# Moving openings, squares and normalising between the slots of a graph-attention layer, and regrouping its first two groups' loads

## The chip, the cores and the metric

The kernel runs on one NeuronCore of a Trainium2 chip. Its engines work from queues of their own, each in order: TensorE (PE in the profile; PEld are its weight loads) does matrix products into PSUM, VectorE (DVE) and ScalarE (ACT) read and write PSUM and SBUF, GpSimd (POOL) works on SBUF only, and SyncE (SP) issues nearly all DMA transfers. The metric is the device time of one execution in microseconds. Three executions before the change took 2890.96, 2896.06 and 2899.04 us; the median is 2896.06. The profiled execution is a fourth one.

## The reference

x has 128 graphs of 128 nodes and 768 features, adj is 128 x 128 x 128. All data are float32.

```python
h = jnp.maximum(_layernorm(x), 0.0)              # over the features, no weights
q, k, v = (split_heads(h @ W + b) for W, b in ((Wq, bq), (Wk, bk), (Wv, bv)))   # 12 heads of 64
scores = einsum('bhqd,bhkd->bhqk', q, k) / sqrt(64) + beta * adj
scores = where(adj > 0, scores, -9e15)
out = einsum('bhqk,bhkd->bhqd', softmax(scores), v)
return x + out
```

## The kernel before

**Groups.** Four graphs make a group; there are 32 groups, 0 to 31. The activations of a group, normalised and transposed (`to_hT`, line 439), lie in six tiles A00 to A12: r (0 or 1) is a pair of graphs, the second digit a third of the features. The weights fall into blocks B00 to B22, and the output of each projection into keys (r, j), two by three. There are three slices of products per group: `qk0` (heads 0 to 5 of q and k), `v`, and `qk1` (heads 6 to 11).

**Group 0** uses plain products (`plain_slice`): 18 slots a slice, each with four products of 256 columns; three slots (k = 0, 1, 2) fill one key, and its PSUM pair is then evicted (line 820 for q and k, line 812 for v, where VectorE adds V's bias). While it runs, VectorE, GpSimd and ScalarE also make the weight sums for the later groups (`prepare`, lines 266 to 296, two steps a slot); each is stored to DRAM (`kept_*`, line 272, SP's queue) from a ring of five buffers, except twelve that stay in SBUF. The raw weights of `qk1` overwrite those of `qk0` in the big tile `sbig`, by eight transfers at V's slot 5 (`raw_qk`). The ring later holds the T tiles that `load_T` (line 319) brings back.

**Groups 1 to 31** use a fast scheme (`product_z`, line 530): 15 products a slice instead of 18, each of seven zones with two halves, from sums of activations (`sum_acts`, line 444, VectorE; `inner`, lines 449 to 451, GpSimd) and the prepared weights T. Products belong to four chains a, b, c, d; a chain accumulates in one PSUM pair, and the running sum is read after each of its products. So the next product of a chain waits for the readings of the one before. The first reading for a key is its *opening*: for q and k three ScalarE instructions (lines 548 and 550), for V five zones by ScalarE (line 544) and then two zones with the bias by VectorE (line 545). Every further reading is a VectorE addition into the key's tile `home` (line 554). When a key is complete, GpSimd decodes it (`decode`): lines 570 to 573 for q and k, 581 to 585 for V.

**Slots.** A slot is one product with what is emitted behind it. The order on every engine is written out by hand: `then(n, f)` puts f behind the product of slot n and ahead of its readings; `then((n, "post"), f)` behind its readings; `trailing` runs between the two; `later(f, s)` defers by s slots. An engine executes its instructions in the order of emission, so an instruction that waits holds back all that were emitted later on that engine.

**What else fills the slots.** `scores` (line 607) multiplies q and k for two heads, VectorE masks (615), ScalarE takes the exponential (617). `attend` (660) multiplies by V; its products are put between the zones of the next slot's product; ScalarE copies (669) and divides (643), VectorE adds x (676). `bias_steps` prepares the mask of the next group in four steps: VectorE transposes adj (467), ScalarE squares it (468) for a range test, VectorE takes the maximum (470) and finishes the mask (472, 473, 475). `norm` (428) is the layer norm's last step on ScalarE, four instructions per graph, from moments that `half_stats` (401) takes on halves of rows that `load_half` (393) loads, and `row_moments` turns through DRAM (413, 417, 418).

**Waiting for the first activations.** For group 1 the moments come from `stats` (344) and two small products (355, 369) in group 0's V slice. For group 2 the eight half rows are loaded and measured from slot 8 of group 0's `qk1` slice to slot 6 of group 1's `qk0` slice, all through one buffer (`if G == 2 or n % 3 == 2`), since the other two lie where group 1's x is kept until then.

Of the kernel before, what the change touches and what calls it, by code (L numbers as in the profile page):

```python
# [17 lines left out]
P = 128  # L18
# [107 lines left out]
def direct(ctx, tc, x, adj, wq, bq, wk, bk, wv, bv, beta, out, bad):  # L126
# [39 lines left out]
    def flat(lo, hi):  # L166
        return sbig[:, lo:hi]
# [36 lines left out]
    ones = const.tile([P, 1], F32, name="ones")  # L204
# [24 lines left out]

    def raw_qk(u, t, parts, engines=(nc.sync, nc.sync)):  # L230
# [5 lines left out]
        for k in range(3):  # L236
            for j in range(3):
                wt[f"qk{u}", f"B{k}{j}"] = v[:, 2 * k:2 * k + 2, :, j]
# [166 lines left out]
    def row_moments(G):  # L405
# [11 lines left out]
        later(lambda: nc.sync.dma_start(turned.rearrange("i b s -> b i s"), t.rearrange("p s g -> p (s g)")), 5)  # L417
        later(lambda: nc.sync.dma_start(to.rearrange("p b s g -> p (b s g)"),
                                        turned.rearrange("i b s -> i (b s)")[None].to_broadcast([NB, SQ, NB * 2 * GRP])), 8)
# [43 lines left out]
    def bias_steps(G):  # L463
# [4 lines left out]
        nc.scalar.activation(raw, raw, AF.Square, scale=beta_s)  # L468
# [45 lines left out]
    def product_z(G, sl, n):  # L514
# [21 lines left out]
        for (r, j), sign in uses:  # L536
            key = (G, sl, r, j)
            op = ALU.add if sign > 0 else ALU.subtract
            if key not in qk:
                left[key] = sum(k == (r, j) for q in PRODUCTS for k, _ in q[3])  # L540
                t = qk[key] = home_qk(*key, zones=True)
                if sl == "v":
                    bias = bv_b[:, j * 2 * P:(j + 1) * 2 * P].rearrange("p (i n) -> p i n", i=2)
                    nc.scalar.activation(t[:, 0:5], p[:, 0:5], AF.Copy, scale=float(sign))
                    nc.vector.tensor_tensor(t[:, 5:7], bias, p[:, 5:7], op)  # L545
# [230 lines left out]
    def plain_slice(G, sl, todo, rows=(0, 1)):  # L776
# [3 lines left out]
        for r in rows:  # L780
            for j in range(3):
# [5 lines left out]
                for at, k in [(at, k) for at in parts for k in range(3)]:  # L787
                    a, b = A[G, f"A{r}{k}"], wt[sl, f"B{k}{j}"]
                    for i in range(2):
                        for c in range(2):  # L790
# [10 lines left out]
                            turn()  # L801
                    if at is not parts[-1]:
# [4 lines left out]
                    if k == 2:  # L807
                        if sl == "v":
                            t = vt[G, sl, r, j] = vring[nv[0] % len(vring)]
                            nv[0] += 1  # L810
                            bias = bv_b[:, j * 2 * P:(j + 1) * 2 * P].rearrange("p (h d) -> p h d", d=HD)
                            nc.vector.tensor_tensor(
                                t.rearrange("p (g h) e -> p g h e", g=2)[:, :, :, 0:HD],
                                bias[:, None, :, :].to_broadcast([P, 2, 4, HD]),
                                p.rearrange("p g (h d) -> p g h d", d=HD), ALU.add)
# [413 lines left out]
```

## Time and profile before

| | |
|---|---|
| median of three runs | 2896.06 us |
| the profiled execution | 2880.61 us, its span 2878.5 us |
| busy: TensorE, VectorE, ScalarE, GpSimd | 2709.7, 2351.4, 1494.1, 2167.5 us |
| DMA | 707.01 MB, mean 246 GB/s, mean share of the engines 82.3% on the main queue |
| granted TensorE clock, mean | 0.993 |
| first product of group 1 | starts at 139.86 us |

Read the table with care: TensorE's 94% is an average over a start in which it often stands and 29 alike groups in which it stands for short, regular gaps. In the groups of lines "idle before" is the time in which an engine stood before that instruction, and the name behind the arrow is what it waited for last. In the stage rows the columns are the stretch, its length, the busy time (and number of instructions) of PE, PEld, DVE, ACT and POOL, the granted clock, the DMA share and GB/s. A row of waits gives the waiting engine, tile and line, what it waited for, the total, the number of times and the longest. A row of the timeline gives start, duration, engine, line, operation, tiles and shape, the number of instructions merged in it, and in brackets the idle time before it and what ended that.

### The profile page before, as it was taken

The page shows a single profiled execution, that of the slowest core. Times are in us where ns is not written, and L with a number is a line of the kernel's source. Part 1 is how long each engine was busy: PE and PEld are TensorE (multiplying, and loading weights), DVE is VectorE, ACT ScalarE, POOL GpSimd, SP SyncE. Part 2 cuts the span into 40 slices and gives each one's busy share as a digit, 9 for nine tenths or more (in the row PEclk, how much of TensorE's full clock was granted, in tenths as well). Part 3 has the DMA queues.
Part 4 walks back from the last instruction along what each step waited for, and adds up shares of the span by engine and source line. Part 5 has one row for each costly group of instructions (what it writes and reads, how often), then busy time and mean ns, then how long its engine had stood idle before and what let it go on. Part 6 is the DMA issues. An engine that isn't in the chain of part 4 may idle for free.

```text
span 2878.5 us, 121298 instructions
## 1 busy us (share of the span) xinstructions
PE 2709.7 (94%) x52005; PEld 2564.9 (89%) x52005; DVE 2351.4 (82%) x3218; ACT 1494.1 (52%) x3812; POOL 2167.5 (75%) x3152
## 2 busy tenths in 40 slices
PE   8789999999999999999999999999999999999998
PEld 7588999999988999889999899999899898999997
DVE  6778888888888788888888888888888888888885
ACT  2256555556454555545565545555555555555644
POOL 3648787778787778777787877787877787777875
PEclk9899999999999999999999999999999999999999
DMA  8688888888888888888888888888888888888875
GB/s 202 197 247 256 242 260 261 254 251 251 242 253 253 257 244 235 258 254 251 254 255 240 257 258 252 256 250 242 257 256 254 247 235 256 261 256 258 238 220 156
DMA packets 543010, 707.01 MB, mean 246 GB/s; under 512 B 107388, under 2 KB 406152, under 8 KB 542472
## 3 DMA queue, kind: packets, MB, share of 16 engines
q1 hardware_dynamic: 541312, 698.45, 82.3%
q8 instruction: 411, 6.73, 0.9%
q10 hardware_dynamic: 1160, 0.79, 0.1%
q14 instruction: 127, 1.04, 0.1%
HBM read 633.51 MB, written 65.59 MB: 243 GB/s over the span
## 4 chain that ended last, share of the span: by engine, by line
PE 42%; POOL 20%; DVE 11%; issue 5%; DMA 2%; ACT 2%; SPq 1%; POOLq 0%; DVEq 0%; ACTq 0%
PE pair L530 34%; DVE home L554 5%; PE pair L607 4%; PE pair L660 4%; POOL v L585 4%; POOL home L583 3%; DMA x<-in_x_dram 2%; POOL v L584 2%; POOL home L582 2%; POOL home L570 2%; POOL v L581 1%; DVE strow L401 1%; POOL A L449 1%; DVE e L615 1%; POOL home L573 1%
## 5 line engine op out<-in xcount | busy, mean ns | idle before, releaser
L554 DVE TENSOR_TENSOR home<-home,pair 128x896 f32<-128x896 f32 x798 | 846.7, 1071 | 202.3 <-PE pair L530 156.6
L530 PE MATMUL pair<-sbig,T_qk 128*64 128x128 f32 x14756 | 954.9, 274 | 16.4 <-ACT e L669 6.8
L530 PEld LDWEIGHTS pair<-sbig,T_qk 128*64 128x64 f32 x14756 | 804.7, 137 | 35.1 <-issue 27.2
L643 ACT ACTIVATE e<-e,sm 128x64 f32<-128x64 f32 x1512 | 382.4, 336 | 289.8 <-DVE sm L631 289.8
L530 PE MATMUL pair<-T_v,sbig 128*64 128x128 f32 x7812 | 458.9, 273 | 3.2 <-DVE home L545 1.4
L530 PEld LDWEIGHTS pair<-T_v,sbig 128*64 128x64 f32 x7812 | 430.5, 137 | 12.8 <-issue 6.2
L660 PE MATMUL pair<-v,e 128*64 128x65 f32 x6048 | 406.5, 222 | 37.3 <-POOL v L585 25.6
L660 PEld LDWEIGHTS pair<-v,e 128*64 128x64 f32 x6048 | 356.6, 137 | 55.4 <-POOL v L585 32.9
L570 POOL TENSOR_TENSOR home<-home 128x256 f32<-128x256 f32 x319 | 307.0, 962 | 65.9 <-DVE home L554 62.9
L449 POOL TENSOR_TENSOR A<-A 128x256 f32<-128x256 f32 x186 | 142.0, 763 | 267.6 <-DVE A L439 267.6
L530 PE MATMUL pair<-A,T_qk 128*64 128x128 f32 x4340 | 337.8, 273 | 5.3 <-issue 5.3
L617 ACT ACTIVATE e<-e 128x1024 f32<-128x1024 f32 x189 | 200.0, 1058 | 230.2 <-DVE e L615 229.9
L530 PE MATMUL pair<-A,res_qk 128*64 128x128 f32 x4340 | 265.6, 273 | 36.6 <-ACT home L550 32.1
L548 ACT ACTIVATE home<-pair 128x640 f32<-128x640 f32 x319 | 224.1, 703 | 134.6 <-PE pair L530 131.8
L530 PEld LDWEIGHTS pair<-A,res_qk 128*64 128x64 f32 x4340 | 238.9, 137 | 44.1 <-ACT home L550 38.6
L428 ACT ACTIVATE x<-x,block 128x192 f32<-128x192 f32 x480 | 231.8, 540 | 81.2 <-DMA x<-in_x_dram 80.3
L573 POOL TENSOR_TENSOR home<-home 128x256 f32<-128x256 f32 x319 | 244.4, 766 | 25.0
L571 POOL TENSOR_TENSOR home<-home 128x256 f32<-128x256 f32 x319 | 237.1, 743 | 25.0
L669 ACT COPY e<-pair 128x520 f32<-128x520 f32 x189 | 111.4, 590 | 256.2 <-PE pair L660 256.2
L530 PEld LDWEIGHTS pair<-A,T_qk 128*64 128x64 f32 x4340 | 237.7, 137 | 7.0 <-issue 7.0
L615 DVE SCALAR_TENSOR_TENSOR e<-pair,biasT 128x1024 f32<-128x1024 f32 x189 | 227.1, 1202 | 4.6 <-PE pair L607 4.2
L572 POOL TENSOR_TENSOR home<-home 128x128 f32<-128x128 f32 x319 | 201.1, 630 | 25.0
(180 smaller groups left out, 4495.2 us busy)
## 6 DMA issues: line engine op xcount, KB each, us to landing
T_qk<-kept_qk SPq DMA_DIRECT2D x682, 448.0 KB
T_v<-kept_v SPq DMA_DIRECT2D x341, 448.0 KB
xo<-in_x_dram SPq DMA_DIRECT2D x189, 256.0 KB
out_dram<-xo SPq DMA_DIRECT2D x189, 256.0 KB
x<-in_x_dram SPq DMA_DIRECT2D x248, 192.0 KB
sbig<-in_x_dram SPq DMA_DIRECT2D x180, 192.0 KB
half<-in_x_dram SPq DMA_DIRECT2D x66, 192.0 KB
kept_qk<-prep_qk SPq DMA_DIRECT2D x22, 448.0 KB
```

The costliest lines, as they stand in the source:

```text
L428: nc.scalar.activation(t, t, AF.Relu, bias=shift[G, n], scale=rstd[G, n])
L530: nc.tensor.matmul(p[q:q + HD, at, :], lhs[:, q:q + HD], rhs, start=(first and at % 4 == 0), stop=True, skip_group_check=True)
L548: nc.scalar.activation(t[:, 0:5], p[:, 0:5], AF.Copy, scale=float(sign))
L554: nc.vector.tensor_tensor(t, t, p[:, 0:7], op)
L570: e.tensor_tensor(t[:, 1:4:2], t[:, 1:4:2], twice(5), ALU.add)
L571: e.tensor_tensor(t[:, 2:5:2], t[:, 2:5:2], twice(1), ALU.add)
L572: e.tensor_tensor(t[:, 4], t[:, 4], t[:, 6], ALU.add)
L573: e.tensor_tensor(t[:, 0:7:6], t[:, 0:7:6], twice(2), ALU.add)
L615: nc.vector.scalar_tensor_tensor(e, ps, SCORE_CAP * ISCALE, bias, op0=ALU.min, op1=ALU.add)
L617: trailing.append(lambda: nc.scalar.activation(e, e, AF.Exp, scale=1.0 / ISCALE))
L643: nc.scalar.activation(o[:, r, b, 0:HD], pa[:, r, b, 0:HD], AF.Copy, scale=t[:, 1, r, b:b + 1])
L660: nc.tensor.matmul(pa[q:q + HD, 2 * g + i, :], k[:, q:q + HD], vt[G, "v", r, h // 4][:, 4 * g + h % 4, :], start=True, stop=True, skip_gro ...
```

## The change

It has three groups of parts.

In every group from 1 on: VectorE's part of V's opening is emitted ahead of ScalarE's; the square of adj goes to `trailing`, behind the slot's openings. In groups 2 to 29, which prepare a next group from the second on: the normalising of graphs 2 and 3 of the next group moves from V's slots 0 to 3 to slots 5, 6, 8 and 9, and the transposition and inner sums of A11 from slot 6 to slot 12. In `qk1` the second and third attend move from slots 7 and 10 to 8 and 11.

In group 0: V's bias comes into PSUM by a product of one row of ones with one row of the bias, two such products per key, and ScalarE evicts by a plain copy; the ones become a 128 x 128 tile. The eight raw loads of `qk1` are issued one a slot, slots 5 to 12. The moments of group 1 move from slots 8 and 10 to 9 and 12, its normalising and first transpositions a slot back.

In groups 0 and 1: group 2's half rows are all loaded and measured in group 1's `qk0` slice, through three buffers, the moments' turn through DRAM follows in fewer slots, and group 2's first two graphs are normalised whole at V's slots 2 and 3.

```diff
-    ones = const.tile([P, 1], F32, name="ones")
+    ones = const.tile([P, P], F32, name="ones")
...
+    def raw_qk1_piece(at):
+        v = flat(0, RAW).rearrange("p (c i n) -> p c i n", c=NC, i=2)
+        a, i = at // 2, at % 2
+        nc.sync.dma_start(v[a * SQ:(a + 1) * SQ, :, i], rows_of[("q", "k")[i]][a][:, :, 3 * P:6 * P])
+        if not at:
+            name_raw(1, flat(0, RAW).rearrange("p (c i j n) -> p c i j n", c=NC, i=2, j=3))
...
-        if G == 2 or n % 3 == 2:
+        if n % 3 == 2:
...
-        nc.scalar.activation(raw, raw, AF.Square, scale=beta_s)
+        trailing.append(lambda: nc.scalar.activation(raw, raw, AF.Square, scale=beta_s))
...
+                    nc.vector.tensor_tensor(t[:, 5:7], bias, p[:, 5:7], op)
                     nc.scalar.activation(t[:, 0:5], p[:, 0:5], AF.Copy, scale=float(sign))
-                    nc.vector.tensor_tensor(t[:, 5:7], bias, p[:, 5:7], op)
...
+                    if sl == "v" and k == 0:
+                        for i in range(2):
+                            nc.tensor.matmul(p[:, i], ones[0:1], bv_b[0:1, j * 2 * P:(j + 1) * 2 * P], start=False,
+                                             stop=True, skip_group_check=True)
...
-                            bias = bv_b[:, j * 2 * P:(j + 1) * 2 * P].rearrange("p (h d) -> p h d", d=HD)
-                            nc.vector.tensor_tensor(
-                                t.rearrange("p (g h) e -> p g h e", g=2)[:, :, :, 0:HD],
-                                bias[:, None, :, :].to_broadcast([P, 2, 4, HD]),
-                                p.rearrange("p g (h d) -> p g h d", d=HD), ALU.add)
+                            nc.scalar.copy(t.rearrange("p (g h) e -> p g h e", g=2)[:, :, :, 0:HD],
+                                           p.rearrange("p g (h d) -> p g h d", d=HD))
...
-        then(12 + g, norm, 1, g)
-    then(5, lambda: raw_qk(1, flat(0, RAW), ((0, 3),)))
+        then(13 + g, norm, 1, g)
+    for n in range(8):
+        then(5 + n, raw_qk1_piece, n)
...
-    then(8, lambda: mom.extend(moments_1(1, 0, GRP * NB)))
-    then(10, lambda: moments_2(1, 0, GRP * NB, *mom))
+    then(9, lambda: mom.extend(moments_1(1, 0, GRP * NB)))
+    then(12, lambda: moments_2(1, 0, GRP * NB, *mom))
...
-    turn_act(1, ((2, "A01"), (3, "A02"), (4, "A00"), (9, "A10"), (10, "A11"), (11, "A12")))
+    turn_act(1, ((3, "A01"), (4, "A02"), (5, "A00"), (9, "A10"), (10, "A11"), (11, "A12")))
...
-    for n, at in enumerate((8, 10, 12, 14, 16)):
-        then((at, "post"), load_half, 2, n)
-    for n, at in enumerate((10, 12, 14, 16)):
-        then(at, half_stats, 2, n)
...
-            for n, at in enumerate((0, 2, 4, 6)):
-                then(at, half_stats, 2, 4 + n)
-                if n:
-                    then((at - 2, "post"), load_half, 2, 4 + n)
-            then(7, row_moments, 2)
+            for n, at in enumerate((0, 0, 0, 3, 4, 5, 6, 7)):
+                then((at, "post"), load_half, 2, n)
+            for n, at in enumerate((3, 4, 5, 6, 7, 8, 9, 10)):
+                then(at, half_stats, 2, n)
+            then(10, row_moments, 2, 3, 5)
...
-            for g in range(2):
-                for h in range(2):
-                    then((2 * g + h, "post"), norm, G + 1, g + (G > 1) * 2, 2 * h, 2 * h + 2)
             if G == 1:
+                for g in range(2):
+                    then((2 + g, "post"), norm, 2, g)
                 turn_act(2, ((5, "A01"), (6, "A00"), (7, "A02"), (14, "A11")))
...
             else:
-                turn_act(G + 1, ((6, "A11"),))
+                for n, at in enumerate((5, 6, 8, 9)):
+                    then((at, "post"), norm, G + 1, 2 + n // 2, n % 2 * 2, n % 2 * 2 + 2)
+                turn_act(G + 1, ((12, "A11"),))
...
-        attention(G, 0, ((3, 2), (7, 1), (10, 0)))
+        attention(G, 0, ((3, 2), (8, 1), (11, 0)))
```

`row_moments` takes the two delays (5 and 8 slots before) as arguments, and `raw_qk`'s naming of the blocks becomes `name_raw`.

More of the change, by code (lines that the diff above doesn't have):

```diff
@@ L228, in load_cols, with name_raw @@
             engine.dma_start(t[a * SQ:(a + 1) * SQ], rows_of[name][a][:, chunks, at:at + t.shape[-1]])
+    def name_raw(u, v):
+        for k in range(3):
+            for j in range(3):
+                wt[f"qk{u}", f"B{k}{j}"] = v[:, 2 * k:2 * k + 2, :, j]
     def raw_qk(u, t, parts, engines=(nc.sync, nc.sync)):
@@ L403, in half_stats, with row_moments @@
             nc.vector.bn_aggr(rows[G, "mv"][:, g, :], rows[G][:, g])
-    def row_moments(G):
+    def row_moments(G, first=5, then=8):
         mv = rows[G, "mv"]
@@ L416, in row_moments @@
         turned = dram.tile([SQ, NB, 2 * GRP], F32, name=f"turned_{G}")
[L417 removed]
+        later(lambda: nc.sync.dma_start(turned.rearrange("i b s -> b i s"), t.rearrange("p s g -> p (s g)")), first)
         later(lambda: nc.sync.dma_start(to.rearrange("p b s g -> p (b s g)"),
[L419 removed]
+                                        turned.rearrange("i b s -> i (b s)")[None].to_broadcast([NB, SQ, NB * 2 * GRP])), then)
         for g in range(GRP):
@@ L1096, in direct @@
     pf = take()
-    nc.tensor.matmul(pf[0:1, 0, 0:NS + 24], ones, over, start=True, stop=True)
+    nc.tensor.matmul(pf[0:1, 0, 0:NS + 24], ones[:, 0:1], over, start=True, stop=True)
     nc.vector.tensor_reduce(bad, pf[0:1, 0, 0:NS + 24], AX.X, ALU.max)
```

4 lines of the change are left out of this document (1 added, 3 removed).

## The prediction

> **What bounds the kernel now.** I read the page first, then the busy time by stages, the waits, and the timeline.
>
> ```profile
> span 2878.5 us, 121298 instructions
> PE 2709.7 (94%) x52005; PEld 2564.9 (89%) x52005; DVE 2351.4 (82%) x3218; ACT 1494.1 (52%) x3812; POOL 2167.5 (75%) x3152
> ...
> PE 42%; POOL 20%; DVE 11%; issue 5%; DMA 2%; ACT 2%; SPq 1%; POOLq 0%; DVEq 0%; ACTq 0%
> ```
>
> TensorE is busy 94%, but the chain that ended last is TensorE for only 42%; 20% is GpSimd. So there is a GpSimd chain inside the groups. The stages, by columns of length, busy time per engine, clock, DMA share:
>
> ```profile
> 0.00:139.80 139.80, 115.55 (x847) 92.12 (x847) 96.77 (x220) 33.75 (x88) 71.85 (x132) 0.94 0.72 196
> 139.80:242.70 102.90, 87.00 (x1645) 83.15 (x1647) 79.83 (x119) 53.20 (x142) 58.26 (x89) 0.92 0.86 254
> 242.70:2772.20 2529.50, 2414.83 (x47682) 2303.38 (x47680) 2107.32 (x2772) 1358.90 (x3455) 1977.04 (x2842) 1.00 0.85 251
> ```
>
> Group 0 takes 139.8 us and group 1 102.9, both with a reduced clock; the 29 groups after them 87.2 each. What waits:
>
> ```profile
> POOL A L449 <- DVE A L439: 267.6, 91, 5.2
> ACT adj L468 <- DVE biasT L467: 266.8, 32, 9.7
> DVE home L545 <- ACT home L544: 160.4, 109, 3.8
> ACT x L428 <- DMA x<-in_x_dram: 80.3, 30, 3.8
> ```
>
> Three of them are queue heads that hold back something else: the square (L468) and the normalising (L428) sit before openings on ScalarE, and L545 keeps VectorE waiting for L544. Where this reaches TensorE, group 14's timeline shows:
>
> ```profile
> 1335.59 0.42 DVE L545 TENSOR_TENSOR home<-bv_b,pair 128x256 f32<-128x256 f32 x1 [2.26 <-ACT home L544]
> 1336.06 1.75 PE L530 MATMUL pair<-res_v,A 128*64 128x128 f32 x28 [0.29 <-DVE home L545]
> 1346.39 0.46 POOL L581 TENSOR_TENSOR v<-home 128x128 f32<-128x128 f32 x1 [3.08 <-DVE home L554]
> 1353.53 0.72 ACT L468 ACTIVATE adj<-adj,beta_s 128x512 f32<-128x512 f32 x1 [9.74 <-DVE biasT L467]
> 1356.53 1.75 PE L530 MATMUL pair<-A,res_qk 128*64 128x128 f32 x28 [1.97 <-ACT home L550]
> 1363.91 1.23 POOL L584 TENSOR_TENSOR v<-sbig 128x128 f32<-128x128 f32 x1
> 1364.85 1.23 DVE L444 TENSOR_TENSOR sbig<-A,sbig 128x896 f32<-128x896 f32 x1
> 1366.72 0.34 PE L660 MATMUL pair<-v,e 128*64 128x65 f32 x4 [0.73 <-POOL v L585]
> 1383.76 0.45 PE L607 MATMUL pair<-home 64*64 64x128 f32 x8 [0.30 <-POOL home L573]
> ```
>
> Marking the start of every product in the timeline and averaging over groups 3 to 29, four gaps beyond the normal pitch stand in each group: 0.95 us before V's slot 7 (1336.06), 1.39 before qk1's slot 3 (1356.53), 1.13 in the attend of qk1's slot 8 (1366.72), and 0.58 in the scores of the next qk0's slot 1 (1383.76). The last two end on GpSimd. From 1346.39 to those scores GpSimd has hardly a pause: 49 instructions, one idle of 0.56 us. The scores end 40.13 us after the start of V's slot 11, with a spread (0.34) half that of the slots before them (0.68): they are locked to GpSimd, whatever TensorE does before.
>
> The start:
>
> ```profile
> 83.65 0.69 DVE L286 TENSOR_TENSOR prep_v<-sbig 128x512 f32<-128x512 f32 x1 [7.50 <-DMA kept_v<-prep_v]
> 102.88 1.12 PE L799 MATMUL pair<-A,sbig 128*64 128x256 f32 x4 [5.94 <-DVE v L812]
> 139.86 2.88 PE L530 MATMUL pair<-sbig,T_qk 128*64 128x128 f32 x28 [4.38 <-DMA T_qk<-kept_qk]
> 149.56 3.26 PE L530 MATMUL pair<-sbig,T_qk 128*64 128x128 f32 x28 [6.82 <-ACT e L669]
> ```
>
> VectorE stands 7.5 us for a kept store queued behind the eight raw loads (issued 68.94 to 72.7), TensorE 5.9 for an eviction in VectorE's queue; group 1 opens with gaps of 4.8 and 7.2 us, and its first product takes 2.88 instead of 1.70.
>
> **The change, part by part.**
>
> *V's opening, VectorE first.* Same two instructions (0.68 on ScalarE, 0.42 on VectorE), still in series, so TensorE's wait for the pair is unchanged: 0. VectorE no longer stands 1.5 us in 127 of 186 openings; behind L545 wait masks (L615) and L554. One gain reaches the chain: before 1346.39 the L545 kept L554 0.28 us late. ScalarE now waits for VectorE's queue; behind it stand exponentials, with three slots (4.6 us) until the next product of that bank.
>
> *Normalising and A11.* Eight L428 (0.54 each) of a group move from V's slots 0 to 3 to slots 5, 6, 8, 9. At slot 0 they waited 2.7 us for x (80.3/30) with the openings of slots 1, 3 and 4 behind; this is what ends the 0.95. I take 0.95 + 0.2 (small gaps at slots 4 and 5) + 0.2 (slot 10 waits for L615) = 1.35 off per group. The price: A11's transposition and its three GpSimd instructions (0.73, 0.46, 0.46, end to end 1.77 with issue) leave slot 6, where GpSimd idled 4 us, for slot 12, inside the unbroken chain. VectorE's 0.70 transposition goes with it; there it is ahead of GpSimd by over 1 us.
>
> *Square behind the openings.* 0.72 us and its wait for the transposition leave the front of qk1's openings: the 1.39 goes. What is late next is GpSimd: TensorE reaches the attend 1.39 us earlier, the attend moves a slot (1.53) later, GpSimd's v is 1.77 - 0.28 later. The wait there is 1.13 + 1.39 - 1.53 + 1.49 = 2.5, against 1.39 + 1.13 = 2.52 before: nothing is won. The maximum over the square (two slots on) still finds it done. With the two attends their xo loads and output stores go a slot back in SP's queue, each past about one T load; xo has three slots and more in hand, so 0.
>
> *Scores of the next qk0.* The chain grows by 1.77, less the idle 0.56, less 0.28: +0.93. Bounds: 0.3 (A11 half covered) and 3.4 (nothing taken up, and two more instructions slowed as below). I take +0.95, nearest the rows. A group: -1.35 + 0.95 = -0.4; 29 groups: **-12**.
>
> At 1363.91 L584 takes 1.23 instead of 0.46 beside L444. [...]
>
> *Group 0.* V's bias: 12 more products of 256 columns, two records each at 0.218 (72 records in 15.70 us): +5.2 on TensorE (bounds 0, if covered, and 24 x 0.30 = 7.2 by the one-column row L1097). Six L812 (0.67) leave VectorE, -4.0; ScalarE gets six copies near L669's 0.59. The larger ones: 0.1 us of GpSimd. Moments a slot and two later: VectorE's dev (74.5 before, about 74.4 now) meets TensorE at 75.5, so the 6.16 and 1.05 gaps go and cover the 5.2. Split loads: the SP queue alternates a raw piece (0.45 us) with a kept store, so the second store no longer lands 10 us late: -7.5 on VectorE, most of the 3.5 at 101.48 too; bounds 0 and 11. A store waiting for GpSimd now holds pieces; the last is wanted from slot 16. ScalarE's last copies stand behind the normalising, about 93; the bank is wanted at 93 to 94. VectorE and GpSimd come about 12 us earlier to their last preparation, and TensorE ends near 124 instead of 135.1. T lands near 129: **-11** (bounds -15 and 0). The normalising and the A0 transpositions, a slot (1.74) later, cost nothing: the normalising waits for shift in any case (12.8 us before), and shift comes about 5 us earlier.
>
> *Group 1.* Five half loads and four statistics leave group 0's end, all eight come to qk0's slots 3 to 10, three slots behind their loads. The waits of L401 (12.8 us) that held L630, L643 and L669 go: 149.56's gap falls to about 3.7. Against it: 2.2 us more on VectorE, and 8.9 MB in 30 us (297 GB/s; 285 was the best stage): 2 to 3 us of late T. The moments' store and load, two slots apart, can hold SP's T loads 2 us once; the ring of five T buffers covers it. Group 2's first normalising, whole at V's slots 2 and 3, stands ahead of openings with one more slot for the moments to land: 0 to +1. qk1's slot 3 wait (3.37) mostly goes. Of 15.7 us over a normal group I take **-7** (bounds -14 and +2).
>
> The granted clock of 0.81 after 139.8 costs group 1 about 1.3 us a product. [...]
>
> Sum: -12 - 11 - 7 = -30. The profiled execution took 2880.61 (span 2878.5 and 2.1), 0.5% under the median 2896.06; 2850.6 by the one is **2866** by the other.
>
> **Rivals.**
>
> *A11 hides* (0.15): GpSimd's 1.77 is covered. For: 267.6 us of L449 waits. Against: those stand elsewhere. A group -0.28 - 1.35 = -1.63, in all -47 - 18 = -65: 2831.
>
> *The start gives nothing* (0.2): ScalarE, now evicting, stands behind L296 and L428 (which waited 15.3 and 12.8 us there), and the 5.2 us of bias show. -12: 2884.
>
> *GpSimd's chain decides, slower* (0.14): 1.77 unreduced and two more L444 overlaps (0.8 each), +3.4 at the scores: 29 x (3.4 - 1.35) = +59, less 18: 2937. It turns from growth above 1.35 + 18/29 = 2.0 us. For: the lock of scores to GpSimd in nearly every group. Against: the 0.56 idle.
>
> **How the numbers follow.** My forecast has 0.48 (its own range 2845 to 2887), 0.03 stays unnamed. 0.3% is about 9 us, what a measurement of this kernel can tell from no change. Faster: nearly all of 0.48, 0.15 and 0.6 of 0.2, about 0.73; same 0.13; slower 0.14. The range 2832 to 2902 leaves about one in ten at each end.
>
> **What would show it.** Right: no gap before V's slot 7 and qk1's slot 3; the attend at slot 9 waiting 2 to 3 us for GpSimd; scores of qk0's slot 1 ending about 41 us after V's slot 11; a group of 86.8; group 1's first product near 129; no 7.5 us wait of L286. Wrong: groups at 85.6 (A11 hidden) or above 88 (chain grown), a first product later than 135, late T in group 1.

## The result, and the profile after

The changed kernel takes 2921.88 us (median; 2920.95 to 2924.34), beside 2893.51 for the kernel before on the same chip: a ratio of 1.0102, with a 95% interval of 1.0075 to 1.0129. It is **1% slower**; forecast was 2866, 1% faster. The profiled execution has a span of 2919.4 us, 40.9 more than the one before.

In this section lines are those of the changed kernel: its products are L540 (L530 before), attends L670 (660), V's decode L591 to L595 (581 to 585), q's and k's L580 to L583 (570 to 573), inner sums L459 to L461 (449 to 451), sums of activations L454 (444). First the page of the changed kernel: span, busy time, chain that ended last.

```profile
span 2919.4 us, 121277 instructions
...
PE 2750.8 (94%) x52029; PEld 2631.6 (90%) x52029; DVE 2343.6 (80%) x3212; ACT 1504.3 (52%) x3818; POOL 2170.9 (74%) x3152
...
PE 71%; POOL 14%; DVE 7%; issue 1%; DMA 1%; ACT 1%; DVEq 0%; POOLq 0%; SPq 0%; ACTq 0%
```

TensorE is "busy" for 41 us more with the same steady products, and its share of the chain rose from 42 to 71%, as if it had got more work. The stages show what stands behind it: group 0, group 1, groups 2 to 30; the column behind POOL's is the granted clock.

```profile
0.00:144.78 144.78, 123.42 (x871) 97.14 (x872) 92.33 (x214) 36.94 (x94) 69.10 (x132) 0.93 0.67 186
144.78:239.71 94.93, 86.64 (x1644) 81.97 (x1646) 79.43 (x121) 52.88 (x141) 58.78 (x91) 0.95 0.93 281
239.71:2814.00 2574.29, 2448.58 (x47682) 2366.15 (x47680) 2103.48 (x2771) 1365.32 (x3453) 1984.17 (x2842) 0.97 0.83 246
```

- Group 0 ends 4.9 us later (144.78 against 139.86); forecast was 11 earlier.
- Group 1 takes 94.9 against 102.9: 8 us off, as forecast (7).
- The 29 steady groups take 2574.29 against 2529.5: 88.77 each instead of 87.22, +45 us in all where -12 was forecast, and their clock fell from 1.00 to 0.97.

The waits of the changed kernel (waiting engine, tile and line, what it waited for, total, times, longest):

```profile
ACT home L555 <- DVE home L554: 165.5, 76, 6.0
...
PEld pair L670 <- POOL v L594: 126.0, 30, 4.3
PE pair L670 <- POOL v L594: 118.8, 30, 4.1
```

And the attend's wait in the kernel before:

```profile
PE pair L660 <- POOL v L585: 25.6, 30, 0.9
```

The waits of the square and the normalising are all but gone (4.1 and 5.0 us in all), and the pair of V's openings waits in the other order for as much in all as before (160.4). Grown is TensorE's wait for GpSimd's decode of V: once a group as before, but 4 us each instead of 0.9. Group 14's timeline around it (qk1's slots 8 and 9; merged rows of other lines are left out):

```profile
1374.59 1.19 POOL L460 TENSOR_TENSOR A<-A 128x128 f32<-128x128 f32 x1
...
1375.50 1.23 DVE L454 TENSOR_TENSOR sbig<-A,sbig 128x896 f32<-128x896 f32 x1
1375.86 1.19 POOL L461 TENSOR_TENSOR A<-A 128x128 f32<-128x128 f32 x1
1376.76 1.23 DVE L454 TENSOR_TENSOR sbig<-sbig,A 128x896 f32<-128x896 f32 x1
1377.01 1.30 POOL L591 TENSOR_TENSOR v<-sbig 128x128 f32<-128x128 f32 x1
...
1380.05 1.18 POOL L594 TENSOR_TENSOR v<-sbig 128x128 f32<-128x128 f32 x1
...
1381.29 0.70 PE L670 MATMUL pair<-v,e 128*64 128x65 f32 x8 [4.03 <-POOL v L594]
...
1385.78 1.09 DVE L564 TENSOR_TENSOR home<-home,pair 128x896 f32<-128x896 f32 x1 [4.86 <-PE pair L540]
```

Two things are to be seen. GpSimd's instructions, 0.46 us elsewhere, take 1.2 to 1.3 beside VectorE's sums. And once TensorE is released it works at half speed: 8 records of the attend take 0.70 us instead of 0.40, until 1386. The clock over that stretch, in three windows:

```profile
1375.89:1379.30 3.41, 1.37 (x26) 1.13 (x22) 3.38 (x4) 1.42 (x5) 3.33 (x4) 1.00 0.93 248
1379.30:1386.13 6.83, 4.84 (x62) 4.84 (x64) 1.97 (x3) 0.23 (x1) 6.30 (x9) 0.50 0.73 175
1386.13:1389.54 3.41, 3.41 (x70) 3.41 (x68) 3.38 (x5) 1.08 (x4) 2.43 (x3) 1.00 0.69 215
```

Such a stretch at 0.50 (3.41 or 6.83 us long) follows this wait in every one of groups 2 to 30; before the change no steady group had one. A product at half speed counts as busy for longer, as these records do: that is most of TensorE's additional 41 us (34 of them in the steady groups, 2448.58 against 2414.83). Marking the starts of products as in the prediction, the means over groups 3 to 29 are, before and after: V's slot 6 (the gap before slot 7) 2.49 and 1.54, qk1's slot 2 2.85 and 1.53, qk1's slots 8 and 9 together 5.31 and 10.14. The two gaps that were to go went; the attend that "wins nothing" lost 4.8 us.

### The profile page after: what moved, and what is told of

Its sections match the earlier page's. It is cut to its first block, busy times and chain, and to the rows that moved or that the text cites. A ratio compares the mean times of both kernels' runs of the same rounds, so it can differ in the third digit from the quotient of the medians.

```text
span 2919.4 us, 121277 instructions
## 1 busy us (share of the span) xinstructions
PE 2750.8 (94%) x52029; PEld 2631.6 (90%) x52029; DVE 2343.6 (80%) x3212; ACT 1504.3 (52%) x3818; POOL 2170.9 (74%) x3152
## 4 chain that ended last, share of the span: by engine, by line
PE 71%; POOL 14%; DVE 7%; issue 1%; DMA 1%; ACT 1%; DVEq 0%; POOLq 0%; SPq 0%; ACTq 0%
PE pair L540 59%; PE pair L617 6%; PE pair L670 5%; DVE home L564 2%; POOL v L594 2%; POOL A L460 1%; POOL v L591 1%; POOL A L461 1%; POOL home L583 1%; POOL home L582 1%; DMA sbig<-in_x_dram 1%; POOL A L459 1%; POOL home L581 1%; POOL v L595 1%; POOL home L592 1%
## 5 line engine op out<-in xcount | busy, mean ns | idle before, releaser
L540 PE MATMUL pair<-sbig,T_qk 128*64 128x128 f32 x14756 | 1013.6, 280 | 7.1 <-DMA T_qk<-kept_qk 3.7
L540 PEld LDWEIGHTS pair<-sbig,T_qk 128*64 128x64 f32 x14756 | 820.6, 141 | 24.7 <-issue 18.9
L670 PE MATMUL pair<-v,e 128*64 128x65 f32 x6048 | 429.2, 234 | 119.4 <-POOL v L594 118.8
L670 PEld LDWEIGHTS pair<-v,e 128*64 128x64 f32 x6048 | 389.2, 149 | 132.5 <-POOL v L594 126.0
L540 PE MATMUL pair<-T_v,sbig 128*64 128x128 f32 x7812 | 456.1, 273 | 1.5 <-issue 0.9
L540 PEld LDWEIGHTS pair<-T_v,sbig 128*64 128x64 f32 x7812 | 430.4, 137 | 8.3 <-issue 6.2
L580 POOL TENSOR_TENSOR home<-home 128x256 f32<-128x256 f32 x319 | 268.1, 841 | 98.6 <-DVE home L564 95.1
L540 PE MATMUL pair<-A,T_qk 128*64 128x128 f32 x4340 | 310.1, 273 | 1.7 <-DVE home L564 1.7
L583 POOL TENSOR_TENSOR home<-home 128x256 f32<-128x256 f32 x319 | 255.2, 800 | 25.0
L581 POOL TENSOR_TENSOR home<-home 128x256 f32<-128x256 f32 x319 | 255.2, 800 | 25.0
L540 PE MATMUL pair<-A,res_qk 128*64 128x128 f32 x4340 | 264.1, 273 | 1.2 <-ACT home L560 1.2
L459 POOL TENSOR_TENSOR A<-A 128x256 f32<-128x256 f32 x186 | 137.9, 742 | 159.3 <-DVE A L449 154.2
L591 POOL TENSOR_TENSOR v<-home 128x128 f32<-128x128 f32 x160 | 98.6, 616 | 205.6 <-DVE home L564 205.6
L540 PEld LDWEIGHTS pair<-A,res_qk 128*64 128x64 f32 x4340 | 240.5, 137 | 1.7 <-ACT home L560 1.7
L438 ACT ACTIVATE x<-x,block 128x192 f32<-128x192 f32 x480 | 234.4, 541 | 5.0 <-DMA x<-in_x_dram 5.0
L540 PEld LDWEIGHTS pair<-A,T_qk 128*64 128x64 f32 x4340 | 234.6, 137 | 2.1 <-DVE home L564 1.9
L625 DVE SCALAR_TENSOR_TENSOR e<-pair,biasT 128x1024 f32<-128x1024 f32 x189 | 227.3, 1202 | 4.9 <-PE pair L617 1.5
```

Source lines behind the costliest of these rows:

```text
L438: nc.scalar.activation(t, t, AF.Relu, bias=shift[G, n], scale=rstd[G, n])
L540: nc.tensor.matmul(p[q:q + HD, at, :], lhs[:, q:q + HD], rhs, start=(first and at % 4 == 0), stop=True, skip_group_check=True)
L580: e.tensor_tensor(t[:, 1:4:2], t[:, 1:4:2], twice(5), ALU.add)
L581: e.tensor_tensor(t[:, 2:5:2], t[:, 2:5:2], twice(1), ALU.add)
L583: e.tensor_tensor(t[:, 0:7:6], t[:, 0:7:6], twice(2), ALU.add)
L625: nc.vector.scalar_tensor_tensor(e, ps, SCORE_CAP * ISCALE, bias, op0=ALU.min, op1=ALU.add)
```

## The experiments

| kernel | us | ratio to before, 95% | steady group, us | first product of group 1 |
|---|---|---|---|---|
| before | 2893.5 to 2897.5 | 1 | 87.22 | 139.86 |
| changed | 2921.88 | 1.0102 (1.0075 to 1.0129) | 88.77 | 144.78 |
| norms_back | 2847.29 | 0.9835 (0.9814 to 0.9856) | 86.04 | 145.68 |
| a11_slot9 | 2849.46 | 0.9845 (0.982 to 0.987) | 86.10 | 143.48 |
| attends_later | 2909.19 | 1.004 (1.0019 to 1.006) | 88.72 | 146.67 |
| filled_wait | 2902.76 | 1.0025 (1.0011 to 1.004) | 87.75 | 143.34 |
| filled_half | 2892.17 | 0.9991 (0.998 to 1.0002) | 87.58 | 144.72 |
| sums_later | 2921.73 | 1.0101 (1.0067 to 1.0135) | 87.87 | 144.85 |
| square_only | 2935.4 | 1.0141 (1.0112 to 1.017) | 88.98 | 139.52 |
| bias_vector | 2906.78 | 1.0038 (1.0023 to 1.0052) | 88.70 | 128.78 |
| copy_vector | 2906.28 | 1.0033 (1.0014 to 1.0052) | 88.75 | 129.81 |
| start_unsplit | 2920.91 | 1.0094 (1.0072 to 1.0116) | 88.74 | 140.26 |
| combined | 2810.45 | 0.9709 (0.9683 to 0.9735) | 85.38 | 130.81 |
| combined_sums | 2818.58 | 0.9742 (0.9726 to 0.9759) | 85.66 | 129.97 |

A steady group is the time from the first product of group 2 to that of group 31, by 29, in the profiled execution. A ratio is to executions of the kernel before that were taken beside those of its row; the first row has the range of their medians. "The chain" is GpSimd's unbroken run from V's decode to the next scores; its times below count from the start of V's slot 11, means over groups 3 to 29.

### A11 out of the chain: norms_back

```diff
+            if G > 1:
+                for g in range(2):
+                    for h in range(2):
+                        then((2 * g + h, "post"), norm, G + 1, g + 2, 2 * h, 2 * h + 2)
...
-                for n, at in enumerate((5, 6, 8, 9)):
-                    then((at, "post"), norm, G + 1, 2 + n // 2, n % 2 * 2, n % 2 * 2 + 2)
-                turn_act(G + 1, ((12, "A11"),))
+                turn_act(G + 1, ((6, "A11"),))
```

> The changed kernel with the normalising of graphs 2 and 3 and A11's transposition and inner sums back at V's slots 0 to 3 and 6; all else as changed. Theory 1 (A11 in GpSimd's unbroken chain makes the wait of qk1's slot 9 long, and the long wait halves the clock): that slot falls from 8.6 us to about 2.5 + 1.1 + 1.4 - 1.5 = 3.5, no half clock in the steady groups, V's slot 7 gets its 0.95 back, the next scores wait for GpSimd as before; a group takes 87.0 to 87.3 as before the change, first product of group 1 still near 144.8, about 2885 us. Theory 2 (the later attends, the square behind the openings or VectorE's opening first cost the time by themselves): slot 9 keeps over 6 us and a group stays above 88.3, 2915 us or more.

Waits and steady groups of norms_back:

```profile
PE pair L670 <- POOL v L594: 32.8, 30, 4.1
...
PE pair L670 <- POOL v L595: 13.4, 29, 0.5
```

```profile
242.30:2737.41 2495.11, 2405.14 (x47680) 2302.47 (x47678) 2098.30 (x2771) 1371.62 (x3451) 1964.17 (x2841) 1.00 0.86 254
```

The wait is 1.1 + 0.5 us, the clock 1.00, and the group is 86.04: 2.7 us shorter for this one part undone. Theory 2 is out. (Slot 9 fell to 4.36 us, not to the 3.5 expected; square_only shows why.) The group is also 1.2 us shorter than before the change, where "as before" was expected; so the square, the order of the openings and the later attends are worth something together. The chain accounts for half of it: the fourth decode of q and k in it, which the scores of qk0's slot 1 wait for, ends 39.08 us after slot 11's start against 39.66 (it starts 0.33 earlier, and its idle of 0.56 is gone). The rest is V: with the normalising back in slots 0 to 3, V's slot 6 takes 2.12 against 2.49, slot 9 1.53 against 1.76.

### A11 in GpSimd's idle: a11_slot9

```diff
-                for n, at in enumerate((5, 6, 8, 9)):
+                for n, at in enumerate((3, 4, 5, 6)):
...
-                turn_act(G + 1, ((12, "A11"),))
+                turn_act(G + 1, ((9, "A11"),))
```

> The changed kernel with the normalising at V's slots 3, 4, 5, 6 and A11 at slot 9, where GpSimd idles 3.8 us before its chain. Theory 1: chain as short as before the change, so the wait of qk1's slot 9 is about 1 us, no half clock, the 0.95 before V's slot 7 stays gone; scores end 39.8 to 40.1 us after V's slot 11; a group takes 85.8 to 86.3, in all about 2855 us (29 x 1.2 under the kernel before, and 3 for the start and group 1). Theory 2: a group stays above 88.

Theory 1 holds, the extra gain didn't come: the chain's fourth decode ends at 39.15, but V's slot 6 takes 2.11, not 1.54. The trace of group 14 shows why (L554 and L555 are VectorE's and ScalarE's part of V's opening, L438 the normalising, L625 a mask; other rows are left out):

```profile
1313.39 1.21 DVE L625 SCALAR_TENSOR_TENSOR e<-pair,biasT 128x1024 f32<-128x1024 f32 x1
...
1314.51 0.41 DVE L554 TENSOR_TENSOR sbig<-bv_b,pair 128x256 f32<-128x256 f32 x1
...
1314.95 0.70 ACT L555 ACTIVATE sbig<-pair 128x640 f32<-128x640 f32 x1 [3.92 <-DVE sbig L554]
...
1316.50 0.98 ACT L438 ACTIVATE x<-x,block 128x192 f32<-128x192 f32 x2
...
1317.38 0.68 ACT L555 ACTIVATE home<-pair 128x640 f32<-128x640 f32 x1
...
1318.12 1.75 PE L540 MATMUL pair<-res_v,A 128*64 128x128 f32 x28 [0.26 <-ACT home L555]
```

Two normalisings run at 1316.50 on ScalarE, ahead of the opening of slot 4 (1317.38), which the product of slot 7 waits for. They were emitted in slot 3, but behind its opening, which starts only at 1314.95: it waits for VectorE's part, now first, itself behind a mask. The normalising doesn't wait for x here; it waits in a queue, and then holds the next opening.

### The attend one slot later: attends_later

```diff
-        attention(G, 0, ((3, 2), (8, 1), (11, 0)))
+        attention(G, 0, ((3, 2), (9, 1), (12, 0)))
```

> The changed kernel with qk1's second and third attend at slots 9 and 12 instead of 8 and 11. Theory 1a (half of the loss is the clock that halves once the wait is as long as 4.1 us): the wait, now in slot 10, is 4.1 - 1.5 = 2.6 us, the clock stays at full, and the scores of the next qk0's slot 1 again end just behind GpSimd's chain, 41 to 42 us after V's slot 11; a group takes 86.9 to 87.4, in all about 2872 to 2885 us. Theory 1b (GpSimd's chain alone is the bound and the clock only fills a wait that would be there in any case): what slot 9 gives back shows as a wait of 1.5 us or more at the next scores, and a group stays at 88.3 or more.

```profile
PE pair L670 <- POOL v L594: 74.3, 29, 2.8
...
PE pair L617 <- POOL home L582: 37.0, 18, 2.1
```

The wait is 2.56, as worked out, but the group stays at 88.72 and the clock is halved 9 times at this wait and 20 times at the next scores, where a wait of 2 us for GpSimd appeared (the second row). What the later slot gave back reappears at the scores and pays the clock there: 1b by the time, though by way of the clock. The profiled execution was the slowest of the eight; the median is 11.5 us less, 0.4 a group, and still far above the 2872 to 2885 of 1a.

### The clock by itself: filled_wait and filled_half

```diff
         e = es[G, oc]
+        for n in range(44 if oc == 1 and G else 0):
+            q = n % 2 * HD
+            nc.tensor.matmul(pair[q:q + HD, 1, 0:P], ones[:, q:q + HD], ones, start=True, stop=True,
+                             skip_group_check=True)
```

> The changed kernel with 44 additional products of 64 x 128 ones (2.4 us at 0.055 each), whose results are overwritten, on TensorE just ahead of the first product of qk1's second attend, groups 1 to 30. So TensorE stands idle for 1.9 instead of 4.3 us there, GpSimd's chain is untouched. In the traces of the changed kernel and of the four runs before this one, a clock window of 3.413 us is granted at half speed when TensorE stood for 2.2 us or more of the window before it, and never after less than 2.1. Theory G (the clock gate takes about 2 us a group, GpSimd's chain the rest): no half window in the steady groups, slot 9 from 8.6 to 6.6 us; the next scores then wait for GpSimd again; a group takes 86.7 to 87.4 and the kernel 2865 to 2882. Theory B (the chain alone bounds the group, the clock only fills a wait): a group stays at 88.5 or more.

Each of these products is two records and takes 0.109 us, not 0.055: the 44 take 4.81, cover the whole wait and hold the attend 0.5 us longer than GpSimd. Even so the group falls by 1.0 (0.7 by the medians of the whole kernel), with no half stretch. In filled_half there are 22.

> As filled_wait, but with 22 additional products. In the run with 44 each took 0.109 us, two records, so together 4.81: they filled the whole wait and held the attend 0.5 us longer than GpSimd did. 22 of them are 2.4 us and leave 1.9 idle. Theory G: no half window in the steady groups; slot 9 near 6.8 us, the attend released by GpSimd and not by the products; what is saved of the 0.5 may come back at the next scores, which GpSimd held 0.9 us in the run with 44. A group 87.2 to 87.8, and so 0.9 to 1.5 of the 1.48 a group that the change lost is the clock's. Theory B: a group at 88.5 or more.

Waits (the attend is L674 here) and steady groups of filled_half:

```profile
PE pair L674 <- POOL v L594: 49.1, 29, 1.9
```

```profile
239.20:2778.92 2539.72, 2465.89 (x48956) 2375.16 (x48954) 2109.01 (x2771) 1367.42 (x3452) 1980.54 (x2842) 1.00 0.85 250
```

Useless products that change nothing but TensorE's idle time make the kernel 30 us faster than the changed one (2892.17) and level with the kernel before. Two of the 29 groups still show a half stretch. So of the 1.55 us that a group lost, 1.19 are the clock's, 35 us in 29 groups (30 by the medians of the whole kernel); theory B is out. What stays, 87.58, is 0.36 above the kernel before: there the chain's fourth decode ends at 41.20, 1.54 later than before the change.

### What stretched the chain: sums_later

```diff
-        sums_at(G + 1, ((6, "S1"), (7, "S9"), (8, "S2"), (9, "S6"), (10, "S10")))
+        sums_at(G + 1, ((9, "S1"), (10, "S9"), (11, "S2"), (12, "S6"), (13, "S10")))
```

> The changed kernel with the five sums of activations on VectorE at qk1's slots 9 to 13 instead of 6 to 10. Theory P (what lengthens GpSimd's chain beyond A11's 1.77 is that its instructions run beside these sums, at 1.2 to 1.3 us instead of 0.46): A12's inner sums and the decode of V's (0, 0) run at 0.46 and 0.73, that decode ends 23.2 to 23.5 us after the start of V's slot 11 instead of 25.2, and the attend waits 2.2 to 2.5 instead of 4.1, with the clock halved in some groups at most; a group 86.8 to 87.8, depending on what the later sums slow in the scores' chain. Theory O (the order or the number of GpSimd's instructions sets it): the decode still ends near 25.2 and a group stays at 88.7.

GpSimd's timeline of sums_later, the same instructions of group 14 as above:

```profile
1364.25 0.46 POOL L460 TENSOR_TENSOR A<-A 128x128 f32<-128x128 f32 x1
1364.79 0.46 POOL L461 TENSOR_TENSOR A<-A 128x128 f32<-128x128 f32 x1
1365.21 0.91 POOL L591 TENSOR_TENSOR v<-sbig 128x128 f32<-128x128 f32 x1
...
1367.41 0.46 POOL L594 TENSOR_TENSOR v<-sbig 128x128 f32<-128x128 f32 x1
1367.82 1.65 POOL L595 TENSOR_TENSOR v<-sbig 128x256 f32<-128x256 f32 x1
```

Theory P holds for the chain: without the sums beside them, the inner sums take 0.46, and L594 ends at 22.2 instead of 25.2. L595 now meets the first sum (1.65 instead of 0.73), so the wait is 1.1 for L594 and 0.9 for L595, with little work between; in 11 of the 29 groups that is enough to halve the clock, there or at the scores. The group is 87.87 in the profiled execution, but that is the fastest of four: they lie between 2897 and 2928, with the median where the changed kernel is. So there is no gain. The granted clock of the two longest is 0.976 where the profiled one has 0.986; where in the groups they lost it, no trace shows. For the time the expectation failed; for the mechanism it held: in the pair of traces GpSimd's inner sums (L460, L461) take 0.46 us without VectorE's sums beside them and 1.19 with them.

### The square alone: square_only

```diff
-        nc.scalar.activation(raw, raw, AF.Square, scale=beta_s)
+        trailing.append(lambda: nc.scalar.activation(raw, raw, AF.Square, scale=beta_s))
```

This is in the kernel before (its line numbers; the attend is L660 and V's decode L584).

> The kernel before with one edit, the square of adj behind the openings. By the prediction nothing is won: the 1.39 of qk1's slot 3 goes, the attend in slot 8 waits 1.13 + 1.39 = 2.5 for GpSimd, the next scores stay locked to its chain; a group 86.9 to 87.3. By the clock windows seen so far a wait of 2.5 lies on the edge of 2.2 per window: in some groups it halves the clock and adds 1 to 2 us, a group up to 88.2 and the kernel up to 30 us slower. If the square were free work on TensorE's path, a group would be 85.9 and the kernel 40 us faster.

```profile
PE pair L660 <- POOL v L584: 86.5, 30, 4.3
```

One instruction moved, and the kernel is 1.4% slower, as much as by the whole change or more (the intervals overlap). The gap before qk1's slot 3 goes (2.85 to 1.53), the attend's wait grows from 1.1 to about 3 (2.5 were worked out), a half stretch follows in 23 of the 29 groups, and the group takes 88.98, where at most 88.2 was expected. "Nothing is won" was too good twice. The clock is one part. The other is GpSimd's chain itself: it starts when it did (2.71 us after slot 11's start), and A11 is not in it, but the last instruction of the decode that the attend waits for ends at 23.58 instead of 22.53. With the gap gone, VectorE's first sum starts 18.2 us after slot 11's start instead of 19.5, and the sums fall on that decode and the instructions just ahead of it. In norms_back the first sum starts at 17.9, and the decode ends at 23.26 although the chain starts 0.33 earlier.

### The start: bias_vector, copy_vector, start_unsplit

In bias_vector VectorE adds V's bias as before and the products of one row are gone:

```diff
-                    if sl == "v" and k == 0:
-                        for i in range(2):
-                            nc.tensor.matmul(p[:, i], ones[0:1], bv_b[0:1, j * 2 * P:(j + 1) * 2 * P], start=False,
-                                             stop=True, skip_group_check=True)
...
-                            nc.scalar.copy(t.rearrange("p (g h) e -> p g h e", g=2)[:, :, :, 0:HD],
+                            nc.vector.tensor_tensor(
...
```

> The changed kernel with V's bias in group 0 added by VectorE as before (no one-row product, no eviction by ScalarE); loads split, moments late, all else as changed. Theory S1 (ScalarE's copies of the raw weights stand in its queue behind the six evictions, and VectorE and GpSimd's preparation behind them): the gap of 10 us at 70 to 80 us goes or shrinks below 3, and the first product of group 1 starts between 126 and 134 us instead of 144.8; in all 10 to 18 us less than the changed kernel. Theory S2 (the raw loads issued one a slot come too late, or the moments two slots later do): the first product stays above 140. A group stays at 88.7 in both.

In copy_vector the products stay and only the copy moves:

```diff
-                            nc.scalar.copy(t.rearrange("p (g h) e -> p g h e", g=2)[:, :, :, 0:HD],
+                            nc.vector.tensor_copy(t.rearrange("p (g h) e -> p g h e", g=2)[:, :, :, 0:HD],
...
```

> The changed kernel with the one-row products of V's bias kept in group 0, but their result copied out by VectorE instead of ScalarE. Theory S1 (ScalarE's queue: the six evictions that wait for TensorE stand ahead of its copies of the raw weights): the first product of group 1 starts between 128 and 132 us, as with the bias on VectorE (128.78). Theory S3 (the twelve products, 5.2 us on TensorE by the prediction, cost the time): it starts at 134 or later, 144 if they cost all of it. Steady groups stay at 88.7.

ScalarE's timeline of the changed kernel: L825 is the eviction of V, L306 the copies of raw weights.

```profile
54.63 0.59 ACT L825 COPY v<-pair 128x512 f32<-128x512 f32 x1 [5.59 <-PE pair L809]
...
61.06 0.58 ACT L825 COPY v<-pair 128x512 f32<-128x512 f32 x1 [5.85 <-PE pair L809]
61.54 0.70 ACT L306 COPY res_v<-sbig 128x128 f32<-128x128 f32 x3
67.49 0.58 ACT L825 COPY v<-pair 128x512 f32<-128x512 f32 x1 [5.25 <-PE pair L809]
67.97 0.70 ACT L306 COPY prep_qk<-sbig 128x128 f32<-128x128 f32 x3
```

What hangs on the copy at 67.97 in the same trace: GpSimd, then VectorE, then the first small product of the moments:

```profile
68.75 0.45 POOL L278 TENSOR_TENSOR prep_qk<-prep_qk 128x128 f32<-128x128 f32 x1 [23.70 <-ACT prep_qk L306]
```

```profile
72.31 0.69 DVE L296 TENSOR_TENSOR prep_qk<-sbig,prep_qk 128x512 f32<-128x512 f32 x1 [18.70 <-POOL prep_qk L279]
```

```profile
80.05 0.43 PE L365 MATMUL pair<-st,sbig 128*64 128x32 f32 x4 [9.81 <-DVE st L354]
```

And the same copy, and the first product of group 1, in copy_vector:

```profile
49.09 0.69 ACT L306 COPY prep_qk<-sbig 128x128 f32<-128x128 f32 x3
```

```profile
129.81 3.09 PE L540 MATMUL pair<-sbig,T_qk 128*64 128x128 f32 x28 [4.33 <-DMA T_qk<-kept_qk]
```

The copy comes 19 us earlier, none of the long waits is left, and the first product starts at 129.81, 15 us earlier; with the bias on VectorE as well, at 128.78. S1 holds, S2 and S3 are out. What the twelve products cost is too little to tell: combined and combined_sums, with the start of bias_vector, have 130.81 and 129.97. And start_unsplit, which is bias_vector with all eight raw loads in slot 5:

```diff
     for n in range(8):
-        then(5 + n, raw_qk1_piece, n)
+        then(5, raw_qk1_piece, n)
```

> The kernel called bias_vector (V's bias by VectorE, first product of group 1 at 128.78 us), with all eight raw loads issued in V's slot 5 again. By the prediction the split is worth 7.5 us on VectorE (the wait of the kept store behind the loads), so the first product of group 1 starts near 136; bounds 129 (the split hides, and the later moments or the loads' end decide) and 140 (all 11 us of the start are the split's). Nothing changes in the steady groups.

140.26: the split is worth 11.5 us beside bias_vector (9.5 beside combined), near the upper end of what was given, and all of the gain of the start.

### The cures together: combined and combined_sums

combined is the changed kernel with A11 at V's slot 6, V's bias by VectorE as in bias_vector, and the normalising all ahead of the opening of V's slot 3:

```diff
+            if G > 1:
+                for n, at in enumerate((0, 1, 2, 2)):
+                    then((at, "post"), norm, G + 1, 2 + n // 2, n % 2 * 2, n % 2 * 2 + 2)
...
+                turn_act(G + 1, ((6, "A11"),))
```

> The changed kernel with A11 at V's slot 6 and the normalising of graphs 2 and 3 at V's slots 0, 1, 2, 2, and V's bias in group 0 added by VectorE. The two cures seen apart, 16 us at the first product and 2.5 us a group, should add; and with all eight normalisings emitted before the opening of V's slot 3, none of them stands ahead of a later opening, so the 0.6 before V's slot 7 goes too. First product of group 1 near 129, a group 85.5 to 86.1, in all 2810 to 2833 us. Rival: a shorter start or V slice is taken back by GpSimd's chain, a group stays at 86.2 and the kernel at 2832.

Group 0 and the steady groups of combined:

```profile
0.00:130.81 130.81, 111.86 (x848) 89.32 (x848) 96.81 (x220) 33.84 (x88) 72.08 (x132) 0.97 0.73 206
226.90:2702.84 2475.94, 2398.37 (x47681) 2302.95 (x47679) 2103.28 (x2771) 1369.62 (x3451) 1962.83 (x2840) 1.00 0.87 256
```

It takes 2810.45 us, 2.9% less than the kernel before, and less than with either cure alone (norms_back 2847.29, bias_vector 2906.78). V's slot 6 takes 1.55, the group 85.38, and the clock stays at 1.00. combined_sums moves the sums as in sums_later:

> The kernel called combined, with the five sums of activations at qk1's slots 9 to 13 instead of 6 to 10. In the changed kernel this move ended the decode of V's (0, 0) 3.0 us earlier and the chain up to the scores 1.3 us earlier. If GpSimd's chain still bounds the group, the wait of qk1's slot 9 (1.9 us now) goes, the scores come up to 1.3 us earlier, and a group takes 84.1 to 84.8 instead of 85.4: 2773 to 2793 us. Rival: the sums then stand beside the decodes of q and k and lengthen those by as much; a group stays at 85.2 or more, 2805 us.

The rival holds: the wait of qk1's slot 9 goes (2.46 us for that slot), but the sums now stand beside the decodes of q and k. The fourth still ends earlier (38.0 against 38.7), the fifth later (42.4 against 42.0); qk0's slots 1 and 3 grow from 3.66 and 2.66 to 4.44 and 3.60, and in eight groups the clock halves, nearly always at those scores. 85.66 a group and 2818.58 us: 8 us more than combined.

## Why the prediction was wrong, point by point

In profiled executions the forecast was -30 us and +40.9 came: 71 us between them (57 for the steady groups, 16 for the start, -1 for group 1, -1 for the last group).

- **"The wait there is ... 2.5, against 2.52 before: nothing is won"** is the step that failed, twice. First its size: the working gave GpSimd's v 1.77 - 0.28 = 1.49 us more; the last instruction of that decode came 3.34 later (25.87 against 22.53). A11 was sized right, the chain's earlier start too (0.33). What the prediction read from a row (L584 with 1.23 instead of 0.46 beside L444) but put at nothing in this sum is that GpSimd's instructions take longer beside VectorE's sums: measured against the shortest duration of each, those up to the end of that decode lost 4.1 us, 2.2 before. Some 1.1 of this 1.9 is not A11's: 3.3 are lost in square_only and norms_back too, where the sums come earlier because the 1.39 is gone. The rest came with A11 in the chain. The sum with the right term, 1.13 + 1.39 - 1.53 + 3.34 = 4.33, is near the waits that the rows show (4.0 on average, 4.3 at most). sums_later shows that the sums are the cause.
- Second, the wait was priced as its own length. A wait of 4.3 us costs 35 us more in 29 groups through the clock (filled_half), and waits of 3.1 and 2.6 halve it too, in 23 groups of square_only and 9 of attends_later. So the 2.5 of the forecast would probably not have been free either. Before the change the same loss lay in two pieces, 1.39 (1.32 by the starts of products above) and 1.13, and the clock was never halved there. None of the rivals had this: the prediction has a price of the clock for group 1 alone (0.81 after 139.8).
- **"Scores of the next qk0: +0.95"**: +1.54 where the clock is out of the way (filled_half), inside the bounds of 0.3 and 3.4. **"1.35 off"** in V's slots was 1.19: slots 6 and 9 fell by 0.95 and 0.23, slot 2 rose by 0.28. Together +0.35 a group where -0.40 was forecast; filled_half has +0.36.
- **"The scores are locked to GpSimd"** held in most groups of every kernel whose clock stayed full: the scores end within 0.6 us of the chain's fourth decode in 24 or more of the 27 groups, in combined in 20. In the changed kernel, with its halved clock, they do so in 12. norms_back gains what the chain gains and what V gains, and the square's 1.39 itself nowhere.
- **V's opening, VectorE first: 0.** Right for that pair, and the chain starts 0.33 earlier (0.28 forecast). But a11_slot9 shows a price: the opening's ScalarE half now waits for VectorE's queue, and what stands behind it comes late.
- **"Group 0: -11"** failed at one term: "ScalarE gets six copies near L669's 0.59". They were priced by their duration. Each waits for TensorE's products, and ScalarE's copies of raw weights, which had run 19 us ahead, stand behind them. The rival named ScalarE's queue but the wrong way round (evictions behind copies). With this one term cured, copy_vector starts at 129.81 for a forecast "near 129", and the one-row products show no cost that can be told, where covered was taken. The split, at 7.5 with 11 as its bound, measured 9.5 to 11.5.
- **"Group 1: -7"** was right: -8, and the gap at its second product fell to 3.3 (3.7 forecast).
- The rival "GpSimd's chain decides, slower" had a growth of over 2.0 us as its turning point; the growth was 1.54, and filled_half, with that growth and the late start, is level with the kernel before. Slower came from the clock (with it, the chain ends 2.15 later); that the rival's 2937 lies near 2921.88 is luck.

## What to carry to other kernels

Price a wait that a change makes or merges at its length and, for TensorE, at what the clock does after it: two short waits may be cheaper than their sum in one place (here 1.39 and 1.13 us a group left the clock at 1.00, one wait of 4.3 cost 35 us more than its length in 29 groups), and products put into the gap, even useless ones, can pay (30 us in filled_half). Price an instruction moved into an in-order queue by when its input is ready, not by its duration, and ask what ran ahead in that queue till now (here evictions of 0.58 us, each waiting 5.3 to 5.9 us for TensorE, held a copy of raw weights back by 19 us). A chain that is already unbroken has no cover for what is added, and everything behind the addition meets other neighbours (here V's decode came 3.34 us later where 1.49 was worked out).

## What the runs showed of the hardware that was not expected

- **The clock fell to half only after steps with over 2 us of idle TensorE.** In each of the traces of the kernel before and of the changed one, all half stretches start on one grid with a step of 3.413 us and are multiples of it long, but for the last, which the end of the trace cuts short. I added up TensorE's idle time per step of the grid (wherever two of its matmul records start over 0.25 us apart, that distance less the usual 0.055; from 200 us on, the 1527 steps at full clock of both traces): the most idle time after which the next step stayed at full clock is 2.23 us (changed kernel, step at 843.41), the least after which it was at half 2.26 (changed kernel, step at 1375.89). In the start of the changed kernel 2.10 was enough (step at 89.06), so these traces show no sharp limit. How a wait lies on the grid counted too: before the change a wait of 3.31 us at 217.13, with 1.67 in one step and 1.64 in the next, left the clock at 1.00.
- **Four kernels have groups as long as 26 steps of that grid.** 26 steps are 88.747 us. The four kernels with the 4.3 us wait and their starts 16 us apart (changed, bias_vector, copy_vector, start_unsplit) have groups of 88.77, 88.70, 88.75 and 88.74, with a spread of 0.16 to 0.22 us over groups 3 to 29; before the change the spread was 0.90. In the changed kernel the first half stretches of the steady groups start at 317.76, 406.50 and 495.25 us, 88.75 apart. If a lock to the grid sets this length, a saving elsewhere in the group would not show. That such a lock, and not the length of the work alone, sets 88.75 was not tested by an experiment of its own.
